# Splitting one PSUM bank into two half-bank slots for the sorted expert tiles

## The chip, the cores and the metric

The kernel runs on one core of one Trainium2 chip. The metric is the device time of one launch in microseconds. A launch was timed three times; one further launch was recorded by the hardware profiler, and all line-by-line times below come from that one.

## What is computed

The input x holds 32 images of 128 channels, 56 x 56 pixels each. Two layers follow each other; cut to what matters here:

```python
x = x + conv3x3(sign(group_norm(x)), sign(w)) * Alpha          # layer 0
t = to_tokens(x)                                               # 3136 tokens of 128 values per image
n = layer_norm(t)
t = t + q(n) * sum_over_tokens(k(n) * v(n))                    # layer 1, first half
n = layer_norm(t)
probs = softmax(n @ router_w + router_b)                       # 8 experts
top_p, top_i = top_k(probs, 2); top_p /= sum(top_p)
t = t + sum_j top_p[j] * (n @ expert_w[top_i[j]] + expert_b[top_i[j]])
```

The last line is where the change lies: each token passes through the two experts its router picks, and the two products are mixed with two gates.

## The kernel before, in words

An image's 3136 tokens are 25 chunks of 128 (the last one holds 64), and four chunks are a block of up to 512 columns. Every image goes through the same stages: sign and convolution (`conv`, L559), turning to tokens (`to_tokens`, L586), statistics, the key-value product (`gram`, `kv_1` to `kv_8`), the projection (`project`, L774), and the router (`route_1` to `route_5`). The experts then come in two ways.

*Dense tokens.* For the first 12 chunks of images 0 to 27, and for all chunks of the last four images, all eight experts run: VectorE multiplies the turned tokens by each expert's gate (`gated`, L1050), and TensorE adds eight products up in one PSUM bank (`experts`, L1068).

*Sorted tokens.* The other 13 chunks of images 0 to 27 are sorted by their pair of experts; there are 28 pairs. `places` (L1170 to L1182, 14 to 16 matmuls) counts on TensorE how many earlier rows have the same pair, `count_on` (ScalarE) and `row_numbers` (VectorE, L1202 on) read that, and GpSimd scatters the rows to memory (`scatter`, L1249). Images form groups of 8, 8, 8 and 4 (`GROUPS`). After a group, `list_1` to `list_4` work out which pair each tile of 128 sorted rows belongs to: `list_sum` (L1455) and `list_3` (L1490) are short matmuls whose results VectorE reads. A group then has up to 127 tiles, taken four at a time as a "quad" (`PER = 4`); there are 116 quads, so 464 tiles. A quad goes through:

- `tile_load` (SyncE): four reads of 128 rows each.
- `tile_turn` (TensorE, L1516) and `tile_turned` (ScalarE, L1522): four transposes into one bank, one copy out.
- `tile_experts` (TensorE, L1534), called twice with h = 0 and 1: for each of two tiles, two products with the weights of the two experts, 128 x 128 each. All four results fill one PSUM bank, 512 float32 per partition.
- `tile_first` (ScalarE, L1549): for each of the two tiles, one read of the first product, with scale and bias.
- `tile_second` (VectorE, L1561): for each of the two tiles, one read of the second product, added to the first.
- `tile_out` (VectorE, L1574) adds the rows themselves for the whole quad, and `tile_store` (SyncE) writes it.

Later `gather` (GpSimd, L1319) brings the rows back to their images, `back_turn` (TensorE, L1334) turns them, and they are stored.

The pools take eight PSUM banks: two for convolution and projection (`ps_mm`, tag mm), two for all transpositions (`ps_tr`, tag tr), one for `gram` and the kv products, two for the dense experts, and one (`ps_to`, tag to). In the kernel before, the last one holds the tiles' products, and between them the results of `places`, `list_sum` and `list_3`, one after another.

*What sets the order.* Each stage is a `Step` with a due time, an engine, an estimated time of work, the steps it follows, and the buffers it takes and frees. `in_order` is a greedy planner run while the program is written: it keeps a clock for each engine, counts the slots of each buffer by `ROOM` (`to=1` before), adds `HOP` where a result passes to another engine, and issues the step that can start soonest (among those within 0.3 us of it, the one that is due first). The instructions are then written down in that order, and each engine executes its own in that order. The semaphore waits between engines are put in by the framework from the tiles that instructions read and write, not by the planner; the planner knows nothing of them beyond `after`, `take` and `free`.

Of the kernel before, what the change touches and what calls it, by code (L numbers as in the profile page):

```python
# [44 lines left out]
F32 = mybir.dt.float32  # L45
# [3 lines left out]
AF = mybir.ActivationFunctionType  # L49
ALU = mybir.AluOpType  # L50
# [4 lines left out]
C = 128  # L55
# [9 lines left out]
PER = 4  # L65
WIDE = PER * C
ROW = C + 4
N_PAIR = N_EXP * (N_EXP - 1) // 2
# [13 lines left out]
HOP = dict(PE=0.8, DVE=0.5, ACT=0.5, POOL=0.5, SP=0.5)  # L82
AHEAD = 0.3
ROOM = dict(
    x=3, tok=3, mm=2, tr=2, acc=1, ff=2, to=1, y=3, qs=3, tt=4, bc=4, gt=2, gated=2,
    t_in=3, turned=2, v=3, back=10, sent=2, o=2,
)

# [72 lines left out]
def conv_attn_moe_kernel(  # L161
# [19 lines left out]
    nc = tc.nc  # L181
    n_img, _, height, width = x.shape
# [15 lines left out]
    n_sort = n_ck - N_DENSE  # L198
# [62 lines left out]
    ew_s = const.tile([C, N_EXP * C], F32, name="ew_s")  # L261
# [141 lines left out]
    def prepare_sorted():  # L403
        nc.gpsimd.memset(hot, 0.0)
        nc.vector.memset(count_h, 0.0)
        nc.gpsimd.memset(before, 1.0)
        nc.gpsimd.affine_select(
            before, before, [[1, C]], ALU.is_gt, 0.0, base=0, channel_multiplier=-1
        )
        nc.gpsimd.memset(upto, 1.0)  # L410
        nc.gpsimd.affine_select(
            upto, upto, [[1, N_PAIR]], ALU.is_ge, 0.0, base=0, channel_multiplier=-1
        )

# [8 lines left out]
        p = ps_to.tile([C, 1], F32, tag="to", name="tile_no_ps")  # L423
# [11 lines left out]
    def at(due, key, engine, work, do, *args, after=(), take=(), free=(), delay=0.0):  # L435
        steps[key] = Step(due, key, engine, work, do, args, after, take, free, delay)
# [43 lines left out]
    def plan_image(i: int):  # L480
        s = base(i)
        d = {}
# [125 lines left out]
        for b in range(n_conv):  # L608
# [4 lines left out]
                take=["mm"],  # L613
# [552 lines left out]
        def places():  # L1166


            p = ps_to.tile([C, n_sort + 1, N_PAIR], F32, tag="to", name=f"places_{i}")
            nc.tensor.matmul(p, lhsT=before, rhs=hot, start=True, stop=False)  # L1170
            if not first_of_group:
                for j in range(2):
                    nc.tensor.matmul(
                        p,
                        lhsT=ones_h[:1],
                        rhs=count_h[:1, j].unsqueeze(1).to_broadcast([1, n_sort + 1, N_PAIR]),
                        start=False,
                        stop=False,
                    )
# [67 lines left out]
        def scatter(c):  # L1247
# [14 lines left out]
        )  # L1262
        at(
            s + 133, ("places", i), "PE", 2.1, places,
            after=[("pair_of", i), ("count_rest", i - 1), ("list_1", group - 1)], take=["to"],
        )
        at(s + 135, ("count_rest", i), "DVE", 0.11, count_rest, after=[("count_on", i)])
        at(s + 134, ("count_on", i), "ACT", 0.22, count_on, after=[("places", i)])
        at(
            s + 137, ("row_numbers", i), "DVE", 1.0, row_numbers,  # L1270
            after=[("places", i), ("count_on", i), ("scatter", i - 2, n_ck - 1)],
            free=[("to", ("places", i))],
        )
        at(
            s + 135, ("row_scalars", i), "DVE", 1.1, row_scalars,
# [105 lines left out]
            )  # L1381


    groups = {}

    def alone(key, dma, keep=()):
# [64 lines left out]

    def list_sum(g):
        d = groups[g]
        d["sum"] = ps_to.tile([C, N_PAIR], F32, tag="to", name=f"ends_ps_{g}")
        nc.tensor.matmul(d["sum"], lhsT=ones[:N_PAIR], rhs=d["diag"], start=True, stop=True)  # L1455

    def list_2(g):
# [27 lines left out]
    def list_3(g):  # L1485

        d = groups[g]
        p = ps_to.tile([1, 3, C], F32, tag="to", name=f"list_ps_{g}")
        for j in range(3):
            nc.tensor.matmul(  # L1490
                p[:, j, :], lhsT=d["vals"][:, j : j + 1], rhs=ident, start=True, stop=True
            )
        d["list_ps"] = p
# [28 lines left out]
        nc.scalar.copy(t, d.pop(("turn", q)))  # L1522
        d["turned", q] = t

    def tile_experts(g, q, h):
        d = groups[g]
        t = d["turned", q]
        if h == 0:
            d["cols", q] = [registers(nc.tensor, g, 1 + j, q, (N_EXP - 1) * C) for j in range(2)]
        p = ps_to.tile([C, 2, 2, C], F32, tag="to", name=f"to_{g}_{q}_{h}")  # L1530
        for k in range(2):
            n = 2 * h + k
            for j in range(2):
                nc.tensor.matmul(  # L1534
                    p[:, k, j, :],
                    lhsT=t[:, n * C : (n + 1) * C],
                    rhs=ew_s[:, bass.ds(d["cols", q][j][n], C)],
                    start=True,
                    stop=True,
                )  # L1540
        d["to", q, h] = p

    def tile_first(g, q, h):
        d = groups[g]
        if h == 0:
            d["v", q] = bpool.tile([C, PER, C], F32, tag="v", name=f"v_{g}_{q}")
        for k in range(2):
            row = d["in", q][:, 2 * h + k, :]
            nc.scalar.activation(  # L1549
                d["v", q][:, 2 * h + k, :],  # L1550
                d["to", q, h][:, k, 0, :],
                AF.Identity,
                bias=row[:, C + 2 : C + 3],
                scale=row[:, C : C + 1],
            )

    def tile_second(g, q, h):
        d = groups[g]
        for k in range(2):
            v = d["v", q][:, 2 * h + k, :]  # L1560
            nc.vector.scalar_tensor_tensor(  # L1561
                v,
                d["to", q, h][:, k, 1, :],
                d["in", q][:, 2 * h + k, C + 1 : C + 2],
                v,
                ALU.mult,
                ALU.add,
            )
        del d["to", q, h]

    def tile_out(g, q):
        d = groups[g]
# [11 lines left out]
    def plan_group(g):  # L1584
# [6 lines left out]
        at(s + 141, ("list_sum", g), "PE", 0.2, list_sum, g, after=[("list_1", g)], take=["to"])  # L1591
        at(
            s + 142, ("list_2", g), "DVE", 1.3, list_2, g,
            after=[("list_sum", g)], free=[("to", ("list_sum", g))],
        )
        at(s + 143, ("list_3", g), "PE", 0.5, list_3, g, after=[("list_2", g)], take=["to"])
        at(
            s + 144, ("list_4", g), "DVE", 0.25, list_4, g,
            after=[("list_3", g)], free=[("to", ("list_3", g))],
        )  # L1600
        for j in range(7):
            at(
# [5 lines left out]
        for q in range(quads_of(g)):  # L1608
# [13 lines left out]
                due + 1, ("tile_turned", g, q), "ACT", 0.47, tile_turned, g, q,  # L1622
                after=[("tile_turn", g, q)], take=["turned"], free=[("tr", ("tile_turn", g, q))],
            )
            for h in range(2):
                at(
                    due + 2 + 2 * h, ("tile_experts", g, q, h), "PE", 0.91, tile_experts, g, q, h,
                    after=[("tile_turned", g, q), ("tile_experts", g, q, h - 1)], take=["to"],
                    free=[("turned", ("tile_turned", g, q))] if h else [],
                )  # L1630
                at(
                    due + 3 + 2 * h, ("tile_first", g, q, h), "ACT", 0.70, tile_first, g, q, h,
                    after=[("tile_experts", g, q, h), ("tile_first", g, q, h - 1)],
                    take=[] if h else ["v"],
                )
                at(
                    due + 4 + 2 * h, ("tile_second", g, q, h), "DVE", 0.53, tile_second, g, q, h,
                    after=[("tile_first", g, q, h)], free=[("to", ("tile_experts", g, q, h))],
                )
            at(  # L1640
                due + 7, ("tile_out", g, q), "DVE", 0.61, tile_out, g, q,
                after=[("tile_second", g, q, h) for h in range(2)] + [("tile_out", g, q - 1)],
                free=[("t_in", ("tile_load", g, q))],
            )
            at(
# [64 lines left out]
```

## Time and profile before

| What | Value |
|---|---|
| median of 3 runs | 2423.75 us (2420.05 to 2426.37) |
| the profiled execution's own time | 2514.33 us |
| span in the profile, first to last instruction | 2512.3 us |
| mean granted TensorE clock in it | 0.967 |
| TensorE matmuls busy | 2247.9 us, 11990 records |
| VectorE busy | 2067.7 us |
| ScalarE busy | 1352.8 us |
| GpSimd busy | 893.4 us |
| DMA | 467.10 MB, mean 186 GB/s |
| first and last product of a sorted tile | 548.3 us and 2280.7 us after the start |

How to read it: the profile's rows name a line of the code, the engine, what is written from what is read, the number of instructions, their busy time with the mean of one, and the idle time of the engine just before them with what ended most of it. A matmul of float32 values has two records, so that the 928 products of sorted tiles are 1856 rows. The profiled execution is 3.7% longer than the median of the plain runs; its durations are compared with its own span.

### The profile page before, as it was taken

To read this page: it belongs to the slowest core of one execution; us is meant where nothing else is said; L and a number is where in the kernel's file an instruction comes from. 1 tells how busy PE (TensorE), PEld (TensorE's weight loads), DVE (VectorE), ACT (ScalarE), POOL (GpSimd) and SP (SyncE) were. 2 spreads that over 40 slices of the span, in tenths; PEclk is the share of its full clock that TensorE was granted. 3 is DMA by queue.
4 is the path that set the end of the run, shared out by engine and by line. 5 is a ranking of instruction groups with operands and counts; after the bars stand their busy time and mean duration, and the time that the engine had idled before them with its cause. 6 is when DMAs were issued, how large, how long until landed. Compare 5 with 4: busy or idle time off the path is not lost. (4 is left out here: it accounts for less than half of the span.)

```text
span 2512.3 us, 44180 instructions
## 1 busy us (share of the span) xinstructions
PE 2247.9 (89%) x11990; PEld 1490.7 (59%) x11990; DVE 2067.7 (82%) x6703; ACT 1352.8 (54%) x4211; POOL 893.4 (36%) x844
## 2 busy tenths in 40 slices
PE   5899999998987989999897889999899897979887
PEld 2666666666665666656665666656666665655543
DVE  4899999998976887998887789989878896768754
ACT  5756665556545654665565566556656634443310
POOL 1043223321221013554432334666542325323542
PEclk9999999999999999999998999999999999999889
DMA  4255554565644554666565456567656666756577
GB/s 153 68 174 193 200 176 165 172 204 181 190 130 146 172 173 135 217 212 195 185 195 166 145 187 205 195 200 234 214 166 193 207 204 212 221 170 219 177 251 239
DMA packets 309734, 467.10 MB, mean 186 GB/s; under 512 B 61129, under 2 KB 209009, under 8 KB 309490
## 3 DMA queue, kind: packets, MB, share of 16 engines
q1 hardware_dynamic: 285186, 414.11, 51.6%
q0 software_dynamic: 23296, 46.64, 6.1%
q10 hardware_dynamic: 1008, 3.54, 0.4%
q8 instruction: 100, 1.64, 0.3%
q14 instruction: 144, 1.18, 0.2%
HBM read 345.73 MB, written 118.39 MB: 185 GB/s over the span
## 5 line engine op out<-in xcount | busy, mean ns | idle before, releaser
L1068 PE MATMUL ff<-gated,ew_d 128*128 128x512 f32 (+1 forms) x1792 | 848.9, 599 | 24.0 <-DVE gated L1050 21.5
L1249 POOL DMA_INDIRECT rows<-tok,row_no x364 | 457.1, 1256 | 963.7 <-issue 298.4
L1319 POOL DMA_INDIRECT back<-res,res_no x364 | 426.8, 1172 | 626.5 <-PE back_ps L1334 263.3
L1050 DVE TENSOR_TENSOR gated<-tt,bc 128x1024 f32<-128x1024 f32 (+1 forms) x448 | 526.6, 1181 | 73.7 <-PE ff L1068 48.8
L1068 PEld LDWEIGHTS ff<-gated,ew_d 128*128 128x128 f32 x1792 | 320.1, 195 | 282.1 <-issue 217.9
L559 PE MATMUL cv<-xs,w_bin 128*128 128x448 bf16 x2016 | 445.1, 363 | 8.2 <-DVE x L570 4.8
L1534 PE MATMUL to<-ew_s,turned 128*128 x1856 | 272.3, 288 | 100.6 <-DVE v L1561 49.1
L1549 ACT ACTIVATE v<-to,t_in 128x128 f32<-128x128 f32 x464 | 186.8, 454 | 306.5 <-PE to L1534 215.9
L1534 PEld LDWEIGHTS to<-ew_s,turned 128*128 128x128 f32 x1856 | 244.8, 198 | 179.7 <-issue 92.9
L788 ACT ACTIVATE qs<-q,r 128x136 f32<-128x136 f32 (+1 forms) x800 | 243.7, 385 | 178.2 <-PE q L774 147.4
L559 PEld LDWEIGHTS <-w_bin 128*128 128x128 bf16 x2016 | 199.1, 100 | 189.8 <-issue 48.8
L774 PE MATMUL q<-move,x 128*128 128x144 f32 (+1 forms) x1600 | 254.7, 297 | 13.1 <-issue 4.9
L650 ACT ACTIVATE y<-tok,r 128x128 f32<-128x128 f32 (+1 forms) x800 | 246.8, 396 | 36.2 <-DVE r L471 31.4
L774 PEld LDWEIGHTS q<-move,x 128*128 128x128 f32 (+1 forms) x1600 | 223.3, 195 | 49.6 <-issue 33.8
L659 PEld LDWEIGHTS gram<-y 128*128 128x128 f32 (+1 forms) x1600 | 203.0, 192 | 46.4 <-ACT y L650 21.9
L1561 DVE SCALAR_TENSOR_TENSOR v<-to,t_in,v 128x128 f32<-128x128 f32 x464 | 142.6, 343 | 103.0 <-ACT v L1549 76.6
L659 PE MATMUL gram<-y 128*128 128x129 f32 (+1 forms) x1600 | 217.8, 282 | 6.2 <-ACT y L650 6.0
L599 DVE BATCH_NORM_STATS2 st<-tok 128x6 f32<-128x128 f32 (+1 forms) x800 | 180.7, 277 | 24.6 <-ACT tok L592 22.0
L807 DVE BATCH_NORM_STATS2 st<-tok 128x6 f32<-128x128 f32 (+1 forms) x800 | 184.2, 276 | 0.0
L570 DVE SCALAR_TENSOR_TENSOR x<-cv,alpha_col,x 128x448 f32<-128x448 f32 x224 | 150.8, 674 | 36.2 <-PE cv L559 16.9
L800 DVE TENSOR_TENSOR tok<-tok,qs 128x384 f32<-128x384 f32 (+1 forms) x288 | 148.6, 516 | 31.3 <-ACT qs L788 24.8
L592 ACT COPY tok<-xt 128x512 f32<-128x512 f32 (+1 forms) x224 | 119.0, 553 | 96.3 <-PE xt L586 56.9
(213 smaller groups left out, 2725.4 us busy)
## 6 DMA issues: line engine op xcount, KB each, us to landing
bc<-gp SPq DMA_DIRECT2D x432, 512.0 KB
x<-in_x_dram SPq DMA_DIRECT2D x64, 784.0 KB
t_in<-rows SPq DMA_DIRECT2D x464, 66.0 KB
res<-v SPq DMA_DIRECT2D x116, 256.0 KB
out_dram<-tt SPq DMA_DIRECT2D x108, 256.0 KB
out_dram<-o SPq DMA_DIRECT2D x84, 256.0 KB
gt<-gb SPq DMA_DIRECT2D x324, 24.0 KB
rows<-zeros SPq DMA_DIRECT2D x116, 66.0 KB
```

Of the source, the lines that this page charges most:

```text
L559: nc.tensor.matmul(cv, lhsT=w_bin[:, t, :], rhs=xs[:, b * ROWS + dy : b * ROWS + dy + ROWS, dx : dx + width], start=(t == 0), stop=(t == T ...
L650: nc.scalar.mul(y[:n, j, :C], d["tok"][:n, c, :C], d["r1"][:n, c : c + 1])
L659: nc.tensor.matmul(d["gram"], lhsT=y[:n, j, :C], rhs=y[:n, j, :], start=(c == 0), stop=(c == n_ck - 1),)
L774: nc.tensor.matmul(p[:n, k, :], lhsT=d["x"][:, c * C : c * C + n], rhs=move, start=True, stop=True,)
L788: nc.scalar.mul(qs[:n, k, : C + N_EXP], p[:n, k, : C + N_EXP], d["r1"][:n, c : c + 1])
L807: nc.vector.bn_stats(st2[:n, c, :], d["tok"][:n, c, :C])
L1050: nc.vector.tensor_tensor(g[:, :, :n], d["tt", b][:, :n].unsqueeze(1).to_broadcast([C, 2, n]), d.pop(("bc", b, k))[:, :, :n], ALU.mult,)
L1068: nc.tensor.matmul(d["ff", b][:, :n], lhsT=ew_d[:, e * C : (e + 1) * C], rhs=g[:, j, :n], start=False, stop=(e == N_EXP - 1),)
L1249: dma = nc.gpsimd.indirect_dma_start(out=groups[group]["rows"], out_offset=bass.IndirectOffsetOnAxis(ap=d["row_no"][:n, c - N_DENSE : c - ...
L1319: dma = nc.gpsimd.indirect_dma_start(out=d["back", c][:n, :], out_offset=None, in_=groups[group]["res"][: quads_of(group) * WIDE, :], in_o ...
L1534: nc.tensor.matmul(p[:, k, j, :], lhsT=t[:, n * C : (n + 1) * C], rhs=ew_s[:, bass.ds(d["cols", q][j][n], C)], start=True, stop=True,)
L1549: nc.scalar.activation(d["v", q][:, 2 * h + k, :], d["to", q, h][:, k, 0, :], AF.Identity, bias=row[:, C + 2 : C + 3], scale=row[:, C : C ...
```

## The change

The bank of tag to is taken once, as one tile `to_all` with two halves of 256 float32 each, and a half holds one tile's two products. `tile_experts`, `tile_first` and `tile_second` handle one tile at a time (n = 0 to 3) in place of two, and successive tiles alternate between the halves. The planner is told that tag to has two slots. `places`, `list_sum`, `list_3` and one product of the preparation take a slot of the transpositions' pool (tag tr) instead. The numbers and sizes of matmuls, ScalarE reads, VectorE reads and DMAs stay the same.

```diff
-    x=3, tok=3, mm=2, tr=2, acc=1, ff=2, to=1, y=3, qs=3, tt=4, bc=4, gt=2, gated=2,
+    x=3, tok=3, mm=2, tr=2, acc=1, ff=2, to=2, y=3, qs=3, tt=4, bc=4, gt=2, gated=2,
...
-            p = ps_to.tile([C, n_sort + 1, N_PAIR], F32, tag="to", name=f"places_{i}")
+            p = ps_tr.tile([C, n_sort + 1, N_PAIR], F32, tag="tr", name=f"places_{i}")
...
-            after=[("pair_of", i), ("count_rest", i - 1), ("list_1", group - 1)], take=["to"],
+            after=[("pair_of", i), ("count_rest", i - 1), ("list_1", group - 1)], take=["tr"],
...
+    to_all = ps_to.tile([C, 2, 2, C], F32, tag="to", name="to_all")
+    n_to = 0
...
-        d["sum"] = ps_to.tile([C, N_PAIR], F32, tag="to", name=f"ends_ps_{g}")
+        d["sum"] = ps_tr.tile([C, N_PAIR], F32, tag="tr", name=f"ends_ps_{g}")
...
-        p = ps_to.tile([1, 3, C], F32, tag="to", name=f"list_ps_{g}")
+        p = ps_tr.tile([1, 3, C], F32, tag="tr", name=f"list_ps_{g}")
...
-    def tile_experts(g, q, h):
+    def tile_experts(g, q, n):
+        nonlocal n_to
...
-        p = ps_to.tile([C, 2, 2, C], F32, tag="to", name=f"to_{g}_{q}_{h}")
-        for k in range(2):
-            n = 2 * h + k
-            for j in range(2):
-                nc.tensor.matmul(
-                    p[:, k, j, :],
-                    lhsT=t[:, n * C : (n + 1) * C],
-                    rhs=ew_s[:, bass.ds(d["cols", q][j][n], C)],
-                    start=True,
-                    stop=True,
-                )
-        d["to", q, h] = p
+        p = to_all[:, n_to % 2]
+        n_to += 1
+        for j in range(2):
+            nc.tensor.matmul(
+                p[:, j, :],
+                lhsT=t[:, n * C : (n + 1) * C],
+                rhs=ew_s[:, bass.ds(d["cols", q][j][n], C)],
+                start=True,
+                stop=True,
+            )
+        d["to", q, n] = p
...
-            for h in range(2):
+            for n in range(PER):
                 at(
-                    due + 2 + 2 * h, ("tile_experts", g, q, h), "PE", 0.91, tile_experts, g, q, h,
-                    after=[("tile_turned", g, q), ("tile_experts", g, q, h - 1)], take=["to"],
-                    free=[("turned", ("tile_turned", g, q))] if h else [],
+                    due + 2 + n, ("tile_experts", g, q, n), "PE", 0.45, tile_experts, g, q, n,
+                    after=[("tile_turned", g, q), ("tile_experts", g, q, n - 1)], take=["to"],
+                    free=[("turned", ("tile_turned", g, q))] if n == PER - 1 else [],
                 )
                 at(
-                    due + 3 + 2 * h, ("tile_first", g, q, h), "ACT", 0.70, tile_first, g, q, h,
-                    after=[("tile_experts", g, q, h), ("tile_first", g, q, h - 1)],
-                    take=[] if h else ["v"],
+                    due + 3 + n, ("tile_first", g, q, n), "ACT", 0.35, tile_first, g, q, n,
+                    after=[("tile_experts", g, q, n), ("tile_first", g, q, n - 1)],
+                    take=[] if n else ["v"],
                 )
                 at(
-                    due + 4 + 2 * h, ("tile_second", g, q, h), "DVE", 0.53, tile_second, g, q, h,
-                    after=[("tile_first", g, q, h)], free=[("to", ("tile_experts", g, q, h))],
+                    due + 4 + n, ("tile_second", g, q, n), "DVE", 0.26, tile_second, g, q, n,
+                    after=[("tile_first", g, q, n)], free=[("to", ("tile_experts", g, q, n))],
                 )
```

`tile_first` and `tile_second` lose their loop over two tiles in the same way; the steps of `places`, `list_sum` and `list_3` take and free tag tr where they took and freed tag to.

More of the change, by code (lines that the diff above doesn't have):

```diff
@@ L422, in prepare_sorted @@
         nc.vector.tensor_scalar(pair_row, pair_no, float(region), None, ALU.mult)
-        p = ps_to.tile([C, 1], F32, tag="to", name="tile_no_ps")
+        p = ps_tr.tile([C, 1], F32, tag="tr", name="tile_no_ps")
         nc.tensor.matmul(p, lhsT=before, rhs=ones_h[:, :1], start=True, stop=True)
@@ L1271, in plan_image @@
             after=[("places", i), ("count_on", i), ("scatter", i - 2, n_ck - 1)],
-            free=[("to", ("places", i))],
+            free=[("tr", ("places", i))],
         )
@@ L1523, in tile_turned @@
         d["turned", q] = t
-    def tile_experts(g, q, h):
+    def tile_experts(g, q, n):
+        nonlocal n_to
         d = groups[g]
         t = d["turned", q]
-        if h == 0:
+        if n == 0:
             d["cols", q] = [registers(nc.tensor, g, 1 + j, q, (N_EXP - 1) * C) for j in range(2)]
-        p = ps_to.tile([C, 2, 2, C], F32, tag="to", name=f"to_{g}_{q}_{h}")
-        for k in range(2):
-            n = 2 * h + k
-            for j in range(2):
-                nc.tensor.matmul(
-                    p[:, k, j, :],
-                    lhsT=t[:, n * C : (n + 1) * C],
-                    rhs=ew_s[:, bass.ds(d["cols", q][j][n], C)],
-                    start=True,
-                    stop=True,
-                )
-        d["to", q, h] = p
@@ L1543, in tile_first @@
-    def tile_first(g, q, h):
+        p = to_all[:, n_to % 2]
[9 more added lines that the diff above has]
+        d["to", q, n] = p
+    def tile_first(g, q, n):
         d = groups[g]
-        if h == 0:
+        if n == 0:
             d["v", q] = bpool.tile([C, PER, C], F32, tag="v", name=f"v_{g}_{q}")
[L1547 to L1555, printed above, removed]
@@ L1557, in tile_second @@
-    def tile_second(g, q, h):
-        d = groups[g]
[L1559 to L1569, printed above, removed]
+        row = d["in", q][:, n, :]
+        nc.scalar.activation(
+            d["v", q][:, n, :],
+            d["to", q, n][:, 0, :],
+            AF.Identity,
+            bias=row[:, C + 2 : C + 3],
+            scale=row[:, C : C + 1],
+        )
@@ L1571, in tile_out, with tile_second @@
+    def tile_second(g, q, n):
+        d = groups[g]
+        v = d["v", q][:, n, :]
+        nc.vector.scalar_tensor_tensor(
+            v,
+            d.pop(("to", q, n))[:, 1, :],
+            d["in", q][:, n, C + 1 : C + 2],
+            v,
+            ALU.mult,
+            ALU.add,
+        )
     def tile_out(g, q):
@@ L1590, in plan_group @@
         )
-        at(s + 141, ("list_sum", g), "PE", 0.2, list_sum, g, after=[("list_1", g)], take=["to"])
+        at(s + 141, ("list_sum", g), "PE", 0.2, list_sum, g, after=[("list_1", g)], take=["tr"])
         at(
             s + 142, ("list_2", g), "DVE", 1.3, list_2, g,
-            after=[("list_sum", g)], free=[("to", ("list_sum", g))],
+            after=[("list_sum", g)], free=[("tr", ("list_sum", g))],
         )
-        at(s + 143, ("list_3", g), "PE", 0.5, list_3, g, after=[("list_2", g)], take=["to"])
+        at(s + 143, ("list_3", g), "PE", 0.5, list_3, g, after=[("list_2", g)], take=["tr"])
         at(
             s + 144, ("list_4", g), "DVE", 0.25, list_4, g,
-            after=[("list_3", g)], free=[("to", ("list_3", g))],
+            after=[("list_3", g)], free=[("tr", ("list_3", g))],
         )
@@ L1641, in plan_group @@
                 due + 7, ("tile_out", g, q), "DVE", 0.61, tile_out, g, q,
-                after=[("tile_second", g, q, h) for h in range(2)] + [("tile_out", g, q - 1)],
+                after=[("tile_second", g, q, n) for n in range(PER)] + [("tile_out", g, q - 1)],
                 free=[("t_in", ("tile_load", g, q))],
```

## The prediction, as made before the result was known

> **What bounds the kernel now.** I read the head of the page first, for the engine that has least room:
>
> ```profile
> span 2512.3 us, 44180 instructions
> PE 2247.9 (89%) x11990; PEld 1490.7 (59%) x11990; DVE 2067.7 (82%) x6703; ACT 1352.8 (54%) x4211; POOL 893.4 (36%) x844
> ```
>
> TensorE (PE) has 2247.9 us of work in 2512.3, so 264 us in which it does nothing. The change alters no matmul, so it can only move those 264 us. VectorE (DVE) at 82% has to feed TensorE within them. Second, the page's groups of instructions, for the three lines that use the bank:
>
> ```profile
> L1534 PE MATMUL to<-ew_s,turned 128*128 x1856 | 272.3, 288 | 100.6 <-DVE v L1561 49.1
> ...
> L1549 ACT ACTIVATE v<-to,t_in 128x128 f32<-128x128 f32 x464 | 186.8, 454 | 306.5 <-PE to L1534 215.9
> ...
> L1561 DVE SCALAR_TENSOR_TENSOR v<-to,t_in,v 128x128 f32<-128x128 f32 x464 | 142.6, 343 | 103.0 <-ACT v L1549 76.6
> ```
>
> The products take 11% of the span but own 100.6 of TensorE's 264 idle us, about half of it put down to the VectorE read. Third, the waits, which show that the three engines wait for each other in a ring:
>
> ```profile
> ACT v L1549 <- PE to L1534: 215.9, 113, 9.0
> ...
> DVE v L1561 <- ACT v L1549: 76.6, 63, 5.1
> ...
> PE to L1534 <- DVE v L1561: 49.1, 32, 7.7
> ```
>
> Fourth, the timeline at 863 us, for one turn of the ring:
>
> ```profile
> 863.68 0.79 ACT L1549 ACTIVATE v<-to,t_in 128x128 f32<-128x128 f32 x2
> ...
> 864.50 0.61 DVE L1561 SCALAR_TENSOR_TENSOR v<-to,t_in,v 128x128 f32<-128x128 f32 x2
> ...
> 865.26 1.48 PE L1534 MATMUL to<-ew_s,turned 128*128 x8 [0.68 <-DVE v L1561]
> ```
>
> ScalarE reads two tiles (to 864.47), VectorE starts 0.03 us later and ends at 865.11, and TensorE, idle for 0.68 us, starts 0.15 us after that. With 0.04 us before ScalarE's start, a full return of the bank takes 0.04 + 0.79 + 0.03 + 0.61 + 0.15 = 1.6 us if neither reader has other work in its queue. In the 232 turns of the trace it is 2.2 us in the middle case and 4.7 in one of ten, since both readers take their instructions in turn.
>
> What this costs depends on the TensorE work that the planner put between two users of the bank; I call it cover. I took it from the compiled order, each instruction at the pace the trace shows in unbroken runs (0.86 us for a 512-column float32 product, two records of 0.43; 0.26 for a 128-column one; 0.13 for a transpose; 0.21 for a convolution matmul), and set against it the idle time that the trace shows ahead of each group's first matmul. Returns from products to products: cover under 2.5 us, 40 returns, 39.7 us idle, so 0.99 each; 2.5 to 3, 43 returns at 0.63; 3 to 3.5, 39 at 0.42; 3.5 to 4, 31 at 0.28; 4 to 5, 27 at 0.20; above, 34 at nothing. The sum is 97 us, which agrees with the page's 100.6. After `places` or the lists, 18 returns lost 0.2 us together.
>
> [...] The halves of the change share one bank and all 128 partitions. [...] The trace of before can't show the case, for there each user fills the bank, but it agrees that readers take turns: VectorE starts only after both ScalarE reads (864.50 against 864.47). [...]
>
> **The change part by part.**
>
> *The halves.* The compiled order of the changed kernel settles what the waits are. Of 297 waits of products on a reader, 213 name a reader of the *other* half; so do 259 of ScalarE's reads and 265 of VectorE's. The bank is handed from engine to engine in program order exactly as before. What has changed is the order, because the planner now believes in two slots: the bank goes to TensorE 324 times (232 before, plus 37 times for places, lists and preparation), in 184 groups of two matmuls and 140 of four. Cover has shrunk: under 2 us in 144 of 323 returns, where before it was so in 8 of the 214 from products to products; the middle case goes from 3.2 us to 2.2.
>
> I price the 323. In 134 both readers still read two tiles each: 58 have cover under 2.5 us, 17, 10, 14 and 8 lie in the next classes, 27 above: 58 x 0.99 + 17 x 0.63 + 10 x 0.42 + 14 x 0.28 + 8 x 0.20 = 78 us. The other 189 need less: 40 wait for two ScalarE and one VectorE read, 31 for one of each, 39 for one VectorE read, 30 for one ScalarE read, 49 for other mixes. The trace of before has no such return. Low end: readers at the middle lags that the trace shows (0.04 and 0.12 us): 0.64 us for a ScalarE read, 0.62 for a VectorE read, 1.6 for one of each, 2.0 for two and one; only covers below those lose, and the lost differences add up to 16 us. High end: queues as long as before's; then a return that needs 1.6 us less reading gets before's loss at a cover 1.6 us longer, and the classes give 126 us. Neither is likely, since part of the queueing is there and short reads find it more seldom; I take the middle, 71. So 78 + 71 = 149 us against 97: **+52 us**, between -3 and +107.
>
> *VectorE's queue.* 265 of its 464 reads now also wait for the other half, sometimes for a product that stands behind a 1.9 us convolution in TensorE's queue. Queued behind such a read are `gated` (1.18 us each) and the convolution's addition, for which TensorE waits. Before has no row for it. It can't gain, since each read keeps its own ScalarE wait; at most I give it half of the existing 76.6 us again, some 40. I take +10.
>
> *Places and lists in the transpositions' banks.* 37 more users share two banks with 637 transposition groups. What leaves: products after places lost 0.2 us, and places waited for a read of the bank 4.9 us in all, so at most -5. What comes: reuses with cover under 1.5 us rise from 72 to about 108. A copy returns a bank in 0.04 + 0.59 + 0.15 = 0.8 us with an idle ScalarE; `places` in about 1.3 (0.18 + 0.19 on ScalarE, 0.53 on VectorE, lags). A loss of 0.2 to 0.5 us on 36 is 7 to 18. Net **+5**, between 0 and +18.
>
> *Same work, other instructions.* Stand-alone waits on TensorE fall from 627 to 574 and rise on ScalarE (829 to 934) and VectorE (915 to 959). A TensorE one has a 0.051 us row, so -3 us at most, mostly beside matmuls: nothing. The register loads for the weights' columns still come once a quad, ahead of the first tile. DMAs are the same in number; a quad's load waits for `tile_out` as before, and its store, the gathers and SyncE's queue follow the tiles' pace. I put nothing on them: the product loop has slack there (t_in has three buffers), and if that cover were gone the late loads would show as TensorE waits at L1516, which are 9.4 us now.
>
> Sum in the profiled execution: 52 + 10 + 5 = +67 us of waiting. Not all becomes time: while TensorE stands at the bank, VectorE and ScalarE run ahead, and of the other 167 us that TensorE idles, those for `gated` and the copies shrink. I let a quarter go: +50, so about 2564 for 2514.33. The plain median stands to the profiled time as 2423.75 to 2514.33, 0.964; +50 becomes +48. I state **2470 us** (+1.9%).
>
> **The rivals.** *Faster by finer turns (2400 us).* ScalarE starts after two matmuls, not four, and a return needs 0.6 to 1.6 us in place of 2.2. If the readers' queues are mostly empty when the short reads come, the 189 short returns cost their low end, 16 us; and if the 134 full ones then also meet emptier queues and lose 0.4 us each (54 us), the bank costs 70 against 97, some -25 us. It decides for itself when the short returns average under about 0.1 us (19 us) and VectorE's false waits cost nothing. For it: ScalarE is only 54% busy. Against: 144 covers under 2 us.
>
> *No change (2424 us).* The planner's order moves everywhere, and TensorE is at 89%: stalls at the bank could replace stalls elsewhere one for one. Against: only 21.5 us of TensorE's idling before L1068 is for `gated`, so little is there to replace.
>
> *VectorE blocked (2540 us).* Short returns at the high end (126) and 40 us on VectorE's queue: 78 + 126 - 97 + 40 + 5 = 152 us, three quarters of it at 0.964 is +110. VectorE would become the late engine. For it: 82% busy, and 265 false waits. Against: ScalarE's reads, which it waits for, are short.
>
> That the change doesn't do what it says (two halves in use at once) is not a rival but my main case; that it does is ruled out by the compiled waits.
>
> **How the numbers follow.** My forecast 0.61, with its own range of 2431 to 2520; faster 0.17; no change 0.11; VectorE blocked 0.11. Within 0.3% (7 us) a measurement of this kernel can't tell a difference from none. Faster 0.17, same 0.11, slower 0.72. The range of 2408 to 2525 leaves out roughly half of each outer rival.
>
> **What would show it.** In the profile of the changed kernel the idle time before the products should rise from 100.6 to about 150 us, and the waits should name ScalarE's read (`v`) as their releaser in many more cases than before. VectorE's idle time before its read should rise above 103 us. TensorE's busy time must stay near 2248 us. Idle before L1068 for `gated` should not grow by more than 20 us. I am wrong if idle before the products falls below 97 us, or if it rises and the span does not.

## The result, and the profile after

The changed kernel takes 2495.67 us (median of 4 runs, 2493.0 to 2498.4), the kernel before 2425.06 us beside it (4 runs, 2420.05 to 2429.64): a ratio of 1.0292, 95% interval 1.0267 to 1.0317. It is 71 us slower.

The head of the page of the changed kernel:

```profile
span 2491.3 us, 44271 instructions
PE 2254.1 (90%) x11990; PEld 1497.2 (60%) x11990; DVE 2073.1 (83%) x6703; ACT 1359.5 (55%) x4211; POOL 882.2 (35%) x844
```

Its span agrees with its plain runs. The span of before in the prediction, 2512.3 us, did not: it was 3.7% above them. Subtracting these two pages would make the change a gain of 21 us. So the kernel before was profiled a second time, as the first experiment (`before_again`), and this page is the one to compare with. Its head:

```profile
span 2420.1 us, 44180 instructions
PE 2214.1 (91%) x11990; PEld 1471.2 (61%) x11990; DVE 2063.8 (85%) x6703; ACT 1351.2 (56%) x4211; POOL 901.4 (37%) x844
```

From this to the changed kernel the span grows by 71.2 us: TensorE idles 237.2 us for 206.0 (+31) and is busy 2254.1 for 2214.1 (+40). The same three groups of instructions as in the prediction, in the changed kernel (the columns after the bar are busy us, mean ns of one, idle us just before and what ended most of it):

```profile
L1538 PE MATMUL to_all<-ew_s,turned 128*128 x1856 | 300.6, 294 | 114.1 <-DVE v L1563 71.4
...
L1552 ACT ACTIVATE v<-to_all,t_in 128x128 f32<-128x128 f32 x464 | 194.1, 456 | 263.7 <-PE to_all L1538 238.9
...
L1563 DVE SCALAR_TENSOR_TENSOR v<-to_all,t_in,v 128x128 f32<-128x128 f32 x464 | 148.6, 344 | 116.1 <-ACT v L1552 91.8
```

and in the second profile of the kernel before:

```profile
L1534 PE MATMUL to<-ew_s,turned 128*128 x1856 | 265.6, 284 | 92.5 <-DVE v L1561 43.5
...
L1561 DVE SCALAR_TENSOR_TENSOR v<-to,t_in,v 128x128 f32<-128x128 f32 x464 | 142.4, 342 | 82.5 <-ACT v L1549 72.2
```

TensorE's idle time ahead of the products rose by 21.6 us, VectorE's ahead of its reads by 33.6, and the products' line is busy 35 us longer. Part of these 35 us is only counted: the records of successive matmuls overlap (those of the products last 0.275 us and start 0.112 us apart in the middle case at full clock, in the changed kernel), and a line's busy time includes the overlap of each group with the instruction before it. If each matmul counts only with what it adds after the end of the one before, the products take 265.5 us in the changed kernel and 240.3 in before_again, so 25 us more. Of the waits of the changed kernel, these are the ring's:

```profile
ACT v L1552 <- PE to_all L1538: 238.9, 152, 6.3
...
DVE v L1563 <- ACT v L1552: 91.8, 76, 3.0
...
PE to_all L1538 <- DVE v L1563: 71.4, 60, 4.2
```

The last one had 32 cases in the prediction's profile, 35 in the second one of before, and has 60 now. TensorE's matmuls also wait for ScalarE's read now; in the second profile of before none does (three weight loads do, 4.2 us; 26 in the changed kernel, 24.8 us). And there are waits against the ring's direction, which the second profile of before doesn't have at all: ScalarE for VectorE's read, and VectorE for products.

```profile
PE to_all L1538 <- ACT v L1552: 10.0, 8, 2.8
ACT v L1552 <- DVE v L1563: 17.5, 21, 3.0
DVE v L1563 <- PE to_all L1538: 11.0, 16, 1.6
```

One turn, from the timeline of the changed kernel, shows a half being no slot of its own. I numbered the tiles by counting records; odd and even tiles lie in different halves.

```profile
1953.22 0.34 DVE L1563 SCALAR_TENSOR_TENSOR v<-to_all,t_in,v 128x128 f32<-128x128 f32 x1
1953.60 0.46 ACT L1552 ACTIVATE v<-to_all,t_in 128x128 f32<-128x128 f32 x1 [3.02 <-DVE v L1563]
...
1954.11 0.71 PE L1538 MATMUL to_all<-ew_s,turned 128*128 x4 [2.01 <-ACT v L1552]
```

VectorE reads tile 359. ScalarE's read of tile 360, whose products were ready before 1951, waits 3.02 us for VectorE, read against read, in the other half. TensorE's products of tile 361 belong in the half that VectorE has just left at 1953.56, and yet they wait for ScalarE's read of tile 360 to end at 1954.06. Over the whole trace, 92 groups of products start after over 0.1 us of idle TensorE, 108 us in all; for 55 of them, 63 us, the read that ended last was one of the other half. Nowhere in it do two engines work on the bank at the same time: of all products, ScalarE reads and VectorE reads of the 464 tiles, no two of different engines overlap.

### The profile page after: what moved, and what is told of

Its sections match the earlier page's. It is cut to its first block, busy times and chain, and to the rows that moved or that the text cites. A ratio compares the mean times of both kernels' runs of the same rounds, so it can differ in the third digit from the quotient of the medians.

```text
span 2491.3 us, 44271 instructions
## 1 busy us (share of the span) xinstructions
PE 2254.1 (90%) x11990; PEld 1497.2 (60%) x11990; DVE 2073.1 (83%) x6703; ACT 1359.5 (55%) x4211; POOL 882.2 (35%) x844
## 5 line engine op out<-in xcount | busy, mean ns | idle before, releaser
L1068 PE MATMUL ff<-gated,ew_d 128*128 128x512 f32 (+1 forms) x1792 | 848.1, 599 | 17.6 <-DVE gated L1050 17.2
L1319 POOL DMA_INDIRECT back<-res,res_no x364 | 419.2, 1152 | 588.4 <-PE back_ps L1334 256.2
L1538 PE MATMUL to_all<-ew_s,turned 128*128 x1856 | 300.6, 294 | 114.1 <-DVE v L1563 71.4
L1538 PEld LDWEIGHTS to_all<-ew_s,turned 128*128 128x128 f32 x1856 | 255.2, 198 | 218.5 <-issue 79.3
L1552 ACT ACTIVATE v<-to_all,t_in 128x128 f32<-128x128 f32 x464 | 194.1, 456 | 263.7 <-PE to_all L1538 238.9
L1563 DVE SCALAR_TENSOR_TENSOR v<-to_all,t_in,v 128x128 f32<-128x128 f32 x464 | 148.6, 344 | 116.1 <-ACT v L1552 91.8
L659 PEld LDWEIGHTS gram<-y 128*128 128x128 f32 (+1 forms) x1600 | 209.2, 196 | 51.7 <-ACT y L650 27.1
L659 PE MATMUL gram<-y 128*128 128x129 f32 (+1 forms) x1600 | 223.9, 285 | 12.4 <-ACT y L650 12.3
L599 DVE BATCH_NORM_STATS2 st<-tok 128x6 f32<-128x128 f32 (+1 forms) x800 | 182.1, 276 | 15.8 <-ACT tok L592 15.3
```

Source lines behind the costliest of these rows:

```text
L659: nc.tensor.matmul(d["gram"], lhsT=y[:n, j, :C], rhs=y[:n, j, :], start=(c == 0), stop=(c == n_ck - 1),)
L1068: nc.tensor.matmul(d["ff", b][:, :n], lhsT=ew_d[:, e * C : (e + 1) * C], rhs=g[:, j, :n], start=False, stop=(e == N_EXP - 1),)
L1319: dma = nc.gpsimd.indirect_dma_start(out=d["back", c][:n, :], out_offset=None, in_=groups[group]["res"][: quads_of(group) * WIDE, :], in_o ...
L1538: nc.tensor.matmul(p[:, j, :], lhsT=t[:, n * C : (n + 1) * C], rhs=ew_s[:, bass.ds(d["cols", q][j][n], C)], start=True, stop=True,)
L1552: nc.scalar.activation(d["v", q][:, n, :], d["to", q, n][:, 0, :], AF.Identity, bias=row[:, C + 2 : C + 3], scale=row[:, C : C + 1],)
```

## The experiments

Three theories were set against each other. T1: the bank is still handed from engine to engine, and the planner's belief in a second slot leaves too little work between the hand-overs. T2: places and lists crowd the transpositions' two banks. T3: any new plan of this tightly packed kernel costs as much. "Cover" is, as in the prediction, the TensorE work in the compiled order between two groups of products. Runs that were sent together ran on one chip, with the kernel before beside them; one chip ran the kernel before at 2526 us, the others at 2419 to 2425, so only ratios are compared.

**before_again**: no edit.

> The kernel before, unchanged, for a second profile: the first one's span of 2512 us is 3.7% above its plain runs, while the changed kernel's profile (2491) agrees with its plain runs (2496), so the two can't be subtracted as they are. If the first profile carried stalls of its own, this span is about 2425 us, TensorE's busy time stays near 2248 us, and the idle time before the products is below 100 us: some 50 to 90 us. If profiling really lengthens this kernel, the span is again near 2512 us.

Measured: 2421.84 us, span 2420.1, TensorE busy 2214.1, idle before the products 92.5 us. The prediction's page of before held about 90 us that the kernel does not have on this chip: 58 us of idling and 34 of busy time. One thing sets that page apart. In it ScalarE and VectorE wait 59 and 23 us for something that the profile traces to no instruction of this core and calls "remote"; the largest entry is

```profile
ACT v L1549 <- remote: 23.0, 6, 8.4
```

The four pages from the chip that needs 2526 us have such waits as well (33 to 94 us on ScalarE, 26 to 53 on VectorE), the nine others have none. So the first page probably comes from a chip of that kind; what the waits are stays open.

**places_in_tr**: one part of the change alone.

```diff
-            p = ps_to.tile([C, n_sort + 1, N_PAIR], F32, tag="to", name=f"places_{i}")
+            p = ps_tr.tile([C, n_sort + 1, N_PAIR], F32, tag="tr", name=f"places_{i}")
...
-            after=[("pair_of", i), ("count_rest", i - 1), ("list_1", group - 1)], take=["to"],
+            after=[("pair_of", i), ("count_rest", i - 1), ("list_1", group - 1)], take=["tr"],
```

(and the same for the lists and the preparation's product)

> The kernel before with one part of the change alone: places, the lists and the preparation's product take a slot of the transpositions' pool; the tiles keep their bank for themselves, two tiles at a time. Theory T1 (the bank is still handed from engine to engine, and the planner's belief in a second slot leaves too little work between the hand-overs): 2425 us, within 10. Theory T2 (the places and lists crowd the transpositions' two banks): most of the 70 us, so 2475 to 2495. Theory T3 (any new plan of this tightly packed kernel costs as much): 2450 to 2500.

Measured: 2430.39 for 2422.92 us, 1.0035 (1.0024 to 1.0046), 88.3 us idle before the products. T2 falls: this part costs 8 us here (6 to 11 by the interval).

**planner_one_slot**: the changed kernel with the number of slots put back, and 0.46 for 0.45 us in an estimate (after_replanned has the second alone).

```diff
-ff=2, to=2,
+ff=2, to=1,
...
-"PE", 0.45, tile_experts, g, q, n,
+"PE", 0.46, tile_experts, g, q, n,
```

> The changed kernel with the planner told the truth, that tag to has one slot (and 0.46 instead of 0.45 us as the estimate for a tile's products). Tiles still pass one at a time, on alternating halves; now always TensorE, ScalarE, VectorE in turn, 464 hand-overs to TensorE, of which 149 have under 2 us of other TensorE work between them and 21 under 1.35, where the changed kernel has 144 and some 80 of 323. A return needs 0.04 + 0.45 + 0.03 + 0.34 + 0.15, about 1.0 us, with idle readers. T1 in its narrow form (the false second slot is the cause): 2425 to 2450 us. If instead handling one tile at a time is what costs (twice the hand-overs), 2480 us or more. T2 and T3: 2480 to 2500 us.

Measured: 2434.45 us, 1.0049 (1.0033 to 1.0065). From the page:

```profile
L1538 PE MATMUL to_all<-ew_s,turned 128*128 x1856 | 314.8, 289 | 92.7 <-DVE v L1563 87.3
```

This is T1 in its narrow form. Tiles pass one at a time, on halves, with 464 hand-overs, and 60 of the 71 us are gone; the idle time before the products is that of the kernel before. The products' line is busy even longer (314.8 us) than in the changed kernel. But by what each matmul adds it is 259.9 us; over all lines TensorE is busy 20.8 us longer than in before_again (2234.9 for 2214.1) and idles 8.5 us less (197.5 for 206.0), which makes the 12 us of span. So splitting the groups costs TensorE some 20 us, and most of the 71 need the second slot as well.

**after_replanned**: the changed kernel, 0.46 for 0.45 in the same estimate.

> The changed kernel with 0.46 in place of 0.45 us as the planner's estimate for a tile's products: nothing else changes but the order that follows from it. It tells how much a plan shifted without a purpose moves the time. T1: 2495 us, within 15, since 330 hand-overs and their short covers stay. T3: anything between 2430 and 2530 us.

Measured: 2501.88 us, 1.0323 (1.0307 to 1.0339), 121.7 us idle before the products. The loss stays through a new plan.

**before_replanned**: the kernel before, 0.92 for 0.91 us as the estimate of `tile_experts`.

> The kernel before with 0.92 in place of 0.91 us as the planner's estimate for two tiles' products, and nothing else: how far a plan moved without a purpose carries this kernel. Covers are as before (47 of 225 returns under 2.5 us, 40 of 214 before). The cover theory: a ratio within 1.000 +- 0.005. Theory T3 (any new plan moves the time by per cents): further off than that.

Measured: 2437.83 for 2419.16 us, 1.0079 (1.006 to 1.0097), with 91.1 us idle before the products. A miss for the 0.5% that I gave it: a plan moved without a purpose carries this kernel by 0.8%. T3 holds in that size, and no single difference under 1% proves anything, here or above; 2.9% and 3.2% are beyond it.

**one_bank_ff1** and **two_banks_ff1**: the changed kernel with a bank taken from the dense experts, and the second one with the two slots in two banks.

```diff
-    ps_ff = ctx.enter_context(tc.tile_pool(name="ps_ff", bufs=2, space=PSUM))
+    ps_ff = ctx.enter_context(tc.tile_pool(name="ps_ff", bufs=1, space=PSUM))
...
-ff=2, to=2,
+ff=1, to=2,
```

```diff
-    to_all = ps_to.tile([C, 2, 2, C], F32, tag="to", name="to_all")
+    to_all = [ps_to.tile([C, 2, C], F32, tag=f"to{j}", name=f"to_all{j}") for j in range(2)]
...
-        p = to_all[:, n_to % 2]
+        p = to_all[n_to % 2]
```

> The changed kernel with one bank, not two, for the dense experts (pool and planner alike), so that a bank is free for the next run to use. It is the partner of two_banks_ff1 and says nothing by itself; I expect 2500 to 2560 us, since a dense block's sum can't start until the last one has been read out.

> As one_bank_ff1, from the same plan, but the two half-bank slots lie in two different banks. The planner's belief is now true. T1 (the halves share a bank and so are handed on in turn): 50 to 70 us faster than one_bank_ff1, and the idle time of TensorE before the products falls from over 110 to under 50 us. If sharing the bank is not the cause, the two are within 15 us.

Measured: 2590.7 and 2545.54 us, 1.0259 (1.0213 to 1.0304) and 1.0077 (1.0036 to 1.0119) of the kernel before on that chip. Two banks save 45 us, a little less than I gave. The products' line with one bank:

```profile
L1538 PE MATMUL to_all<-ew_s,turned 128*128 x1856 | 303.7, 297 | 109.1 <-DVE v L1563 79.6
```

and with two:

```profile
L1538 PE MATMUL to_all<-ew_s,turned 128*128 x1856 | 284.4, 288 | 78.7 <-DVE v L1563 48.4
```

The idle time did not fall under 50 us as expected, but by 30, and the products' line is 19 us less busy. In the trace with one bank no two engines overlap on it; with two banks 334 pairs of accesses overlap, all of them in different halves, and ScalarE and VectorE have none of the waits against the ring any more (15.3 and 9.2 us with one bank). The planner's plan is the same in both; the framework, freed of the waits, then placed 671 of the 11990 matmul records elsewhere, so the 45 us are those of sharing the bank with all that follows from it. The second run also makes two tiles of one, so whether the waits go by tile or by bank was not separated; that two reads wait for each other, though neither needs the other's result, speaks for the bank.

**shorter_cover** and **longer_cover**: the kernel before, with only the planner's beliefs changed.

```diff
-"ACT", 0.70, tile_first, g, q, h,
+"ACT", 0.10, tile_first, g, q, h,
...
-"DVE", 0.53, tile_second, g, q, h,
+"DVE", 0.10, tile_second, g, q, h,
```

```diff
                     after=[("tile_first", g, q, h)], free=[("to", ("tile_experts", g, q, h))],
+                    delay=1.5,
```

> The kernel before with the planner's estimates for both readers of the bank cut to 0.1 us each (0.70 and 0.53 before): it now believes that the bank comes back 1 us sooner, and 95 of 215 returns have under 2.5 us of cover, 43 under 2 (before 40 and 8 of 214). Same banks, same two tiles at a time. T1: idle time before the products about 130 us, time 2445 to 2475 us. If short cover doesn't matter, 2425 us within 10.

> The kernel before with one number more: the planner is told that the bank comes free 1.5 us after VectorE's read has ended (a delay on tile_second). The planner then puts more TensorE work between two users of the bank: 13 of 215 returns have under 2.5 us (before 40 of 214), 16 under 3 (before 83). T1 with the table of the prediction: the idle time before the products falls from some 92 to about 50 us, and the time to between 2380 and 2410 us, provided that the plan loses nothing elsewhere. T3: 2400 to 2480, without relation to the cover.

Measured: 2582.12 and 2493.7 for 2526.22 us: shorter 1.023 (1.0193 to 1.0267), longer 0.9886 (0.9847 to 0.9924). So the kernel before loses most of what the change costs if its planner believes in an early bank, without any new tile or slot; and it gains if the planner believes in a late one. The products' line with the longer cover:

```profile
L1534 PE MATMUL to<-ew_s,turned 128*128 x1856 | 266.2, 284 | 48.7 <-DVE v L1561 26.5
```

48.7 us of idling, as the table of the prediction gave it (50). With the shorter cover:

```profile
L1534 PE MATMUL to<-ew_s,turned 128*128 x1856 | 273.8, 288 | 100.2 <-DVE v L1561 51.9
...
PE l L1023 <- ACT tt L1030: 30.6, 4, 14.7
```

This is 100.2 us, not the 130 expected, though the time rose as expected. The first page of before, the nearest in kind (both have "remote" waits, 145 us in this one and 82 in the first), has 100.6. So that the loss arises at the bank is not shown here: what grew is TensorE's idle time before L1023, 47.2 us for 17.3, where it waits for ScalarE's copies. The edit isn't pure either: it also makes the planner believe that ScalarE and VectorE are done with their work earlier. The delay of the other runs leaves the engines' work as it is; but with it the planner also holds `tile_out`, which follows on the same engine, back by that time. What that does alone was not tried.

**cover_half_us**: as longer_cover, with `delay=0.5`.

> The middle dose of longer_cover: in the kernel before, the planner is told that the bank comes free 0.5 us after VectorE's read (1.5 us there). 14 of 225 returns have under 2.5 us of cover, 58 under 3. By the cover theory about two thirds of longer_cover's gain over the kernel before (1.1% there): a ratio of 0.990 to 0.995, and some 65 us idle before the products. A plan that has moved without a purpose would give anything from 0.99 to 1.01.

Measured: 2402.14 for 2419.16 us, 0.993 (0.9913 to 0.9948), 67.3 us idle before the products. It is faster than both kernels, by 17 us than the one before; alone, this is no more than a purposeless plan may do. The products' line:

```profile
L1534 PE MATMUL to<-ew_s,turned 128*128 x1856 | 263.6, 283 | 67.3 <-DVE v L1561 34.4
```

Idle time before the products follows the dose, though on three chips: 92.5, 67.3 and 48.7 us for 0, 0.5 and 1.5 us.

**one_slot_longer**: planner_one_slot, with `delay=1.0` on `tile_second`.

> The changed kernel with the planner told of one slot, as in planner_one_slot, and of a bank that comes free 1.0 us after VectorE's read. Returns with under 2 us of cover fall from 149 of 463 to 67. The cover theory: idle time before the products falls from 93 to about 60 us and the ratio to the kernel before from 1.005 to 0.985 to 0.995, no better than longer_cover, since 464 short groups of products keep TensorE busy some 49 us longer than 232 long ones.

Measured: 2546.47 us, 1.0536 (1.0518 to 1.0554). A clear miss, with the idle time at 85.4 us. The waits name another place:

```profile
PE to_all L1538 <- DVE v L1563: 81.1, 84, 6.2
PE back_ps L1334 <- DMA back<-res,res_no: 67.5, 52, 9.8
```

TensorE waits 67.5 us for gathered rows (18.6 in before_again). The tile view of the products has the last one at 2459.8 us (2333.7 in planner_one_slot, 2190.3 in before_again), with the dense work done by then. The likely account: with 464 turns, each believed to take a microsecond longer, the planner stretched the sorted tiles until they set the end. From 2200 us to the end the granted TensorE clock is 0.76, where before_again has 0.91. By this account, cover is worth having only while the bank's turns fit into the time of a group. (The 49 us of the expectation are the products' line with its overlaps; what the short groups really add is the 20 us above.)

**two_slots_longer**: the changed kernel itself, with one line more.

```diff
                     after=[("tile_first", g, q, n)], free=[("to", ("tile_experts", g, q, n))],
+                    delay=1.5,
```

> The changed kernel itself (two half-bank slots in one bank, places in the transpositions' banks, planner told of two slots) with one number more: a slot comes free 1.5 us after VectorE's read. The hand-overs to TensorE fall from 324 to 269, and those with under 2 us of cover from 144 to 31. If the short covers between falsely independent slots are what the change costs, the ratio to the kernel before falls from 1.029 to between 0.995 and 1.010, with some 60 to 80 us idle before the products (114 in the changed kernel). If something else in the change costs the 70 us (places among the transpositions, tiles handled singly), it stays above 1.02.

Measured: 2415.85 for 2419.98 us, 0.9985 (0.9974 to 0.9996).

```profile
L1538 PE MATMUL to_all<-ew_s,turned 128*128 x1856 | 274.5, 286 | 74.3 <-DVE v L1563 33.6
```

With every part of the change in place and longer covers, the whole 2.9% is gone, as expected, and the products' line is busy 274.5 us instead of 300.6: most groups of products are then four again (195 of the 269 times that the bank goes to TensorE; 140 of 324 in the changed kernel). This step of 3% is about four times what a purposeless plan did.

## Why the prediction was right, and where it was off

*The mechanism.* Right, and shown: the halves do not work side by side (no overlap in the changed kernel, 334 in two_banks_ff1; the turn at 1953 us); the cost comes with the planner's belief and its short covers (planner_one_slot, two_slots_longer). In the kernel before, too, the planner's belief about the bank alone moves the time (longer_cover, shorter_cover), but there the loss was not seen at the bank. That the bank passes from engine to engine as one, the prediction had from the compiled waits, and the trace bears it out down to read against read: ScalarE's 3.02 us behind VectorE's read, one of 21 such waits of 17.5 us in all. (VectorE's start at 864.50 after ScalarE's end at 864.47, in the trace of before, doesn't tell: that read needs ScalarE's result anyway.) The prediction looked for ScalarE's read as releaser in "many more cases"; it is so for 8 matmuls and 26 weight loads (none and 3 in before_again), so the sign came, but VectorE's read stays the main releaser with 60 matmuls. What the chip does when two engines use one bank at once was not shown: neither the changed kernel nor one_bank_ff1 has an overlap on the tiles' bank.

*The size: 48 us forecast, 71 measured.* Three terms of the sum were off, in opposite directions, so that the forecast comes as near as it does is partly luck: 67 us of waiting and no busy time were forecast, 31 us of idling and 40 of busy time came.

- "+52 us" idle before the products: measured +21.6 (92.5 to 114.1). Of the forecast 149 us, 78 were for returns where both readers read two tiles; in the trace these lost 48. The rest was given 71 and lost 60. There the 39 returns behind a single VectorE read have 9 stalls of 7 us together, and the 30 behind a ScalarE read 4 of 6 us, so these were cheap; but some 40 behind two ScalarE and one VectorE reads lost 36 us. The prices per return came from the first page of before, the slow one.
- "TensorE's busy time must stay near 2248 us": at 2254.1 it seems to, but against the right profile it rose by 40 us. I had counted matmuls as unchanged and put nothing on their time. Their number is unchanged, but their groups are smaller, more of them start behind idle time, and more of them run at half clock.
- The quarter that I let go, as stalls covered elsewhere, and the factor 0.964. Nothing was covered: TensorE's idle time away from the bank rose too, by 9.6 us. The factor carried the slow page over to the plain runs.

The clock was left out of the sum altogether:

```profile
core 0: 2491.3 us, clock 0.969
```

before_again has:

```profile
core 0: 2420.1 us, clock 0.979
```

The granted clock is either full or half in the traces: by these mean clocks, half for 154 us of the changed kernel, and for about 102 before. TensorE was busy in 135 and 84 us of this. In the changed kernel the records of 128x512 float32 products start 0.43 us apart at full clock and 0.85 at half. With half the work done at half clock, the difference costs 25 of the 40 us (an estimate from these numbers), and 15 are left to the smaller groups.

What comes before the half clock? All changes of the clock in the trace of the changed kernel lie on a grid of 3.41 us, so I compared stretches of that length. Mostly, a drop is not preceded by a single gap as long as that. In the 34 stretches of 3.41 us right before a drop to half, TensorE idled all through in one; the longest gap was 2.1 us in the middle case. What the stretches share is that stalls add up: TensorE was busy for under 60% in 32 of the 34, and in only 23 of the 650 other stretches at full clock. Of the 75.7 us of idling in the 34, 45.1 lie before the products; before_again has 23 such stretches, with 22.4 of 51.1 us before the products. So the added drops go with the added stalls at the bank. That is read from the traces; no run changed the one without the other.

*VectorE's queue, +10 us.* That readers wait behind other work in their queues is seen in the trace of before: all 6703 VectorE records start in the order of the compiled program, and of the 310 us between what the first ScalarE and VectorE reads of the 232 turns wait for and their starts, the reader was at other instructions for 215. VectorE's idle time ahead of the reads rose from 82.5 to 116.1 us, above the 103 named as a sign. TensorE's wait for `gated` fell from 20.0 to 17.2 us; the rival with VectorE blocked did not occur.

*Places and lists, +5 us (0 to 18).* 8 us in places_in_tr, within what a purposeless new plan does.

*The rivals.* Finer turns and no change: both excluded by the interval. planner_one_slot, which hands every tile over alone, gains nothing either at 1.0049. T3, which I had as "the order moves everywhere", is worth 0.8% in before_replanned.

*The profile used.* The base of the sum came from an execution 3.7% too long. The table of idle by cover held nevertheless (97 us, 92.5 in the second profile), but the reading "busy unchanged" and the factor 0.964 did not. One statement in the description of the kernel is too strong as well: engines don't keep the planner's order fully; the framework moves some instructions, as the 671 records show.

What stays open is what the "remote" waits of some executions are, where the loss of shorter_cover comes from, and whether the clock would have dropped without the stalls at the bank.

## What to carry to other kernels

Two slots that the engines really used at once, in two banks, were 45 us faster than two in one bank (two_banks_ff1 against one_bank_ff1, 334 overlaps against none). Two tiles in one PSUM bank were handed from engine to engine as one (no overlap in the changed kernel), and the planner's belief in two slots then packed the hand-overs closer than the readers could follow (114.1 us idle before the products, for 92.5). Before the change is made, compile it and look which reader each wait names. A planner's estimate of when a buffer comes back is worth setting from the trace, with the queues of the readers in it: 1.5 us more on one step took back the whole 2.9% here (two_slots_longer), and 1.0 us more in a ring turned 464 times lost 5% (one_slot_longer).

## What the runs showed of the hardware

How soon a waiting matmul started depended on the number of reads before it more than on the engine that read: 0.055 us after a single VectorE read (94 of 96 cases in planner_one_slot), 0.146 us after the second of two (66 of 67 in before_again), 0.05 us after a ScalarE read (8 of 8 in the changed kernel). The 0.15 us that the prediction put on every return holds for pairs only. A group of products that starts behind idle time adds more to TensorE's busy time than one that follows another instruction directly: two products of 128 x 128 float32 add 0.76 for 0.49 us in the changed kernel, four 1.20 for 0.93 in before_again (means at full clock). Nearly every drop of the clock to half followed 3.41 us in which TensorE was busy for less than 60%, mostly without a gap of that length (32 of 34 drops in the changed kernel, 20 of 23 in before_again); but 23 of 55 such stretches in the changed kernel had no drop behind them. And one and the same kernel took 2419 to 2425 us on some chips and 2526 us on another: a profile is to be compared with the plain runs beside it before it is used as a base.
